# Fifteen of sixteen centroid rows in the table products of layers 1 and 2, and the attention weights loaded after the branch

## The chip, the cores and the metric

The kernel runs on one core of a Trainium2 chip. A core has five engines that run side by side, each through its own list of instructions in order: PE (TensorE, matrix products into PSUM), DVE (VectorE), ACT (ScalarE), POOL (GpSimd) and SP (SyncE, which here issues nearly all DMA transfers). They meet only at semaphores. The metric is the device time of one execution in microseconds (us). Before the change the median of three runs is 3867.28 us (3863.39 to 3868.2).

## The reference

The input x is 32 images of 1024 channels, 14 x 14 = 196 positions. Layer 0 is `x + L0(gn(x))`, and L0 is a chain of three table convolutions, each followed by a batch norm:

```python
scores = 2.0 * einsum('blcs,cks->blck', v, centroids) - sum(centroids * centroids, -1)
attn = softmax(scores * inv_temp, axis=-1)          # over the k = 16 centroids
out = einsum('blck,cko->blo', attn, lut)            # c codebooks, 16 table rows each
```

The first has 256 codebooks of 4 channels and 256 outputs, the second 256 codebooks of 9 values (the 3 x 3 neighbourhood of one channel) and 256 outputs, the third 64 codebooks of 4 channels and 1024 outputs. The 16 attention weights of a codebook add up to 1, so the sum over the 16 weighted table rows equals the last row plus the first fifteen weights times (row minus last row). The part that is the same at every position is taken out again by the mean in the batch norm that follows:

```python
m = x.mean((0, 2, 3), keepdims=True)
return g[None, :, None, None] * (x - m) * rsqrt(v + EPS) + b[None, :, None, None]
```

A second part, `x + L1(gn(x))`, is linear attention with rotated queries and keys and a 3 x 3 depthwise convolution. Everything is float32.

## The kernel before, in words

**Units.** Images go in NP = 16 pairs, 392 positions each. A unit is 64 codebooks of one pair: 4 blocks j of 128 rows (8 codebooks x 16 centroids), 8 units b to a pair, 128 units u = 8p + b to a layer. `units` (L626) is the loop of layers 1 and 2. In iteration i the program writes, in this order:

- `score(i + ahead)`: four score products on PE (L780 in layer 1; L897 and L906 in layer 2), and `exponentials` (L558) on ACT, which write the unit's tile t;
- `token_major` for the unit before that: DVE turns t into tt (L570); in layer 1 POOL adds its halves (L573);
- `softmax`: DVE sums (L587), inverts (L589) and turns the inverse back into r (L595), and POOL scales t by r (L596). In layer 1 (`halve`) this is unit i + 2, since ahead is 4; in layer 2 it is unit i + 2 as well, since ahead is 3;
- `side(i)`: what else is due in this iteration, from a list by iteration number;
- `lut(i)`: eight products on PE (L640), two halves h of the outputs times four blocks j, added up over the eight units of a pair. Each is two PE records.

Each engine keeps this order. The tiles t lie in a ring of ahead + 2 (`unit_tiles`, L616): six in layer 1, five in layer 2; unit u uses tile u modulo the ring's length.

**SP's queue.** Layer 1 loads x of a later pair (L247) once in eight units. In layer 2, `score2` issues the twelve patch loads of the next half pair (`load_patches`, L845) before the first unit of every four, into the one of two buffers that the last score products have left; `store_pair` (L825) writes six pieces of the padded activations once in eight units. A transfer that waits for a semaphore holds back all that follow it on SP.

**Tables.** `load_lut` fills one of eight tiles of 128 x 1024 (L237). Layer 1's are loaded at the start, layer 2's as the last pair of layer 1 leaves them, layer 3's likewise. After layer 3 the same tiles take the attention weights, wk (four tiles, the keys) and wq, in `projections`, called as `weights4` ahead of the branch.

**The branch.** The fast layers leave out the softmax's maximum; `overflow` (L602 to L608) checks that no sum left its range, and `tc.If(again > 0)` (L1036) repeats the layers exactly if one did. All engines meet there. With this input it isn't taken.

**The attention part** is written by a planner, `Plan`: each piece has an engine, a rank, an estimated duration and what it reads and writes, and at each free moment of an engine the ready piece of the lowest rank is emitted. `load` has the pieces for x (L1157) and for the third layer's output o3d (L1172); for the first pair the two x halves and the o3 pieces of half 1 were loaded before the branch (`given`). `front` and `group_norm` (L1192 to L1260) prepare the inputs, `channels` (L1318) multiplies by wk and wq.

Of the kernel before, what the change touches and what calls it, by code (L numbers as in the profile page):

```python
# [10 lines left out]
F32 = mybir.dt.float32  # L11
AF = mybir.ActivationFunctionType
ALU = mybir.AluOpType
# [4 lines left out]
P = 128  # L18
# [132 lines left out]
def conv_preact_kernel(ctx: ExitStack, tc: tile.TileContext, a: dict, out: bass.AP):  # L151
# [80 lines left out]
    def load_lut(b, src):  # L232

        v = weights[b]
        if len(src.shape) == 3:
            v = v.rearrange("p (s w) -> p s w", s=src.shape[1])
        nc.sync.dma_start(v, src)  # L237
        return v
# [120 lines left out]
    def score_biases(ps_tr, pool, tmp, i, raw, rows, groups, mask, per, order=None):  # L359
# [43 lines left out]

    lut1_rows = lambda b: a["lut1"][b * 512 : (b + 1) * 512].rearrange("(s q) w -> q s w", q=P)


    lut2_rows = lambda b: a["lut2"].rearrange("(h j b q) w -> h b q j w", h=2, j=4, q=P)[
        b // 4, b % 4
    ]

# [7 lines left out]
    def attention_inputs(stack):  # L418
# [61 lines left out]

        def projections(_):
            for b in range(8):
                t = a["wkT" if b < 4 else "wqT"]
                load_lut(b, t[(b % 4) * P : (b % 4 + 1) * P])

        return [loads, third, tables], projections, [third, projections]


    def layers(exact, early=None):
# [126 lines left out]
        def unit_tiles(pool, ahead):  # L616
# [6 lines left out]
            return ts  # L623

        def units(ahead, ts, pool, luts, score, bias, dst, stats, side, last, halve=False):

            n = 8 * NP
            po, late, tts = [], [], {}  # L630

            def lut(u):
                p, b = divmod(u, 8)
                if b == 0:
                    po[:] = [
                        ps_po.tile([P, 512], F32, tag="po", name="po")[:, :N2] for h in range(2)
                    ]
                order = [(h, j) for h in range(2) for j in range(4)]
                for h, j in order if b == 7 else sorted(order, key=lambda k: k[1]):
                    nc.tensor.matmul(  # L640
                        po[h],
                        luts[b][:, j, h * P : (h + 1) * P],
                        ts[u % len(ts)][:, j, :N2],
                        start=(b == 0 and j == 0),
                        stop=(b == 7 and j == 3),
                    )
                if b == 7:
                    for h in range(2):
                        o = dst[:, h, p * N2 : (p + 1) * N2]
                        nc.scalar.copy(o, po[h])  # L650
                        late.append((stats[:, h, p, :], o))

            for i in range(-ahead, n):
                u = i + ahead
                if u < n:
                    scs = score(u)
                    exponentials(ts[u % len(ts)], scs, bias[:, 4 * (u % 8) :][:, :4])
                u = i + ahead - 1
                if 0 <= u < n:
                    tts[u] = token_major(pool, ts[u % len(ts)], halve)  # L660
                u = u - 1 if halve else u
                if 0 <= u < n:
                    softmax(pool, u, ts[u % len(ts)], *tts.pop(u))
                while late:
                    nc.vector.bn_stats(*late.pop(0))
                side(i)
                if i >= 0:
                    lut(i)
            for h in range(2):
                nc.vector.bn_stats(*late.pop(0))  # L670
                last(h)
# [4 lines left out]
        with ExitStack() as s:  # L676
# [54 lines left out]

            luts2 = []

            def next_lut(b):
                return lambda: luts2.append(load_lut(b, lut2_rows(b)))

# [3 lines left out]
            at(24, edges)  # L740
            at(40, masks2)
            for b in range(7):
                at(8 * (NP - 1) + b + 1, next_lut(b))

            for p in range(2):
                xts[p] = load_x(xp, p)
            luts = [load_lut(b, lut1_rows(b)) for b in range(8)]
            if not exact:
                masks()
                load_consts(True)  # L750
            for i in (2, 3):
                load_raw(i)
            load_raw2()
            bias1, biases = score_biases(ps_tr, once, st, 1, raw[1], P, CT, mask8, 4)
# [19 lines left out]
            def score1(u):  # L774
# [12 lines left out]
                st,  # L787
                luts,
                score1,
# [6 lines left out]
            )  # L796
            next_lut(7)()
            add_up(0, 8 * NP)


        with ExitStack() as s:
            once = s.enter_context(tc.tile_pool(name="p2c", bufs=1))
            st = s.enter_context(tc.tile_pool(name="p2tt", bufs=1 if exact else 2))
            luts, luts3 = luts2, []

# [32 lines left out]
            def load_patches(n, b0=0, m=4):  # L838
                p, h = divmod(n, 2)
                for j in range(4):  # L840
                    for r0, dy, k in TAPS:
# [8 lines left out]
                        )  # L850

            store_pair(0, 0)
            load_patches(0, 0, 1)
# [63 lines left out]
            def side2(i):  # L917

                p = {1: 1}.get(i + ahead, (i + ahead + 9) / 8)
                if p in range(1, NP):  # L920
                    for h in range(2):
                        store_pair(int(p), h)
                if i == 60:
                    bias3, biases = score_biases(ps_tr, big, st, 3, raw[3], P, 2, mask8, 4)
                    parts[3] = score_matrices(big, 3, "", raw[3], mask8), bias3
                    biases()
                next_lut3(i - 8 * (NP - 1) - 1)

            def next_lut3(b):
# [9 lines left out]
                st,  # L939
                luts,  # L940
                score2,
# [89 lines left out]
    with tc.manual_schedule(engines=engines):  # L1031
        again = layers(False, early)
        weights4(None)

# [11 lines left out]
    with ExitStack() as s:  # L1046
# [102 lines left out]
        def load(p, h, rank):  # L1149
# [17 lines left out]
            for k in range(2):  # L1167
                ot = Slot("o3q")
                q = 2 * h + k

                def third(ot=ot, q=q):
                    nc.sync.dma_start(ot(), o3d[:, 2 * q : 2 * q + 2, p * N2 : (p + 1) * N2])  # L1172

                if p == 0 and h == 1:
                    ot.ap = given[f"o3_{k}"]
                else:
                    do(SP, rank - 11 + 8 * k, 0.45, third, (), [(ot, 0), (ot, 1)], lag=4.5)
                os.append(ot)
            return xt, os

        def front(p, h, c, xt, ot, rank):
# [34 lines left out]
            do(DVE, rank, 0.54, added, [w], [xk])  # L1216
            do(DVE, rank, 0.56, stats, [xk], [("gst", p % 2, h, c)])

        def group_norm(p, h, rank):
# [35 lines left out]
            def middle():  # L1255
# [11 lines left out]
            do(PE, rank, 0.3, average(pv, g("gq")), [key("gq")], [pv], lag=0.3)  # L1267
            do(DVE, rank, 0.1, variance, [pv], [key("gve")])
            do(
                POOL, rank, 1.9, scale, [key("gve"), key("nmc")], [key("ga"), key("gb")], port=True  # L1270
# [38 lines left out]
        def channels(p, keys, j, r, t, sums, rank):  # L1309
# [3 lines left out]
            pv = lambda: pq()[:, :N2]  # L1313

            def product():
                m0 = r * 512 + j * P
# [30 lines left out]
            done = ["wk"] if keys and p == NP - 1 else []  # L1347
            do(PE, rank, 2.76, product, ys_ + done, [pq, *held], lag=0.25)
            do(ACT, rank - 20, 0.49, relu, [pq], [e])
# [307 lines left out]
        def pair(p, t):  # L1657
# [51 lines left out]
            for n, j in enumerate(js):  # L1709
# [17 lines left out]
                if n % 2:  # L1727
                    store(p, j // 2, xts[j // 2], t + T + 40 + 20 * n)

        for p in range(NP):  # L1730
            pair(p, T * p)
# [74 lines left out]
```

## Time and profile before

| what | value |
|---|---|
| median of three runs | 3867.28 us |
| the profiled execution's own time | 3861.88 us |
| its span (first to last instruction) | 3860.0 us |
| PE busy | 3715.2 us, 96% |
| DVE busy | 3002.4 us, 78% |
| POOL busy | 2300.7 us, 60% |
| ACT busy | 1687.7 us, 44% |
| mean granted PE clock | 0.985 of full speed |

The instructions of layer 1 lie between 8 and 859 us of the span, those of layer 2 between 860 and about 1896, those of layer 3 up to 2665, then come the branch and the attention part. In the profile, L640 is line 640 of the kernel; `t<-t,lut` names the tiles written and read; a bracket at a line's end tells how long the engine was idle before it and what released it. Issuing a transfer does not count as busy time of SP. Several equal instructions in a row are merged in the timeline (x4), and the time given is from the first's start to the last's end. A busy PE is not a PE at its peak, as ends of products are modelled.

### The profile page before, as it was taken

To read this page: it belongs to the slowest core of one execution; us is meant where nothing else is said; L and a number is where in the kernel's file an instruction comes from. 1 tells how busy PE (TensorE), PEld (TensorE's weight loads), DVE (VectorE), ACT (ScalarE), POOL (GpSimd) and SP (SyncE) were. 2 spreads that over 40 slices of the span, in tenths; PEclk is the share of its full clock that TensorE was granted. 3 is DMA by queue.
4 is the path that set the end of the run, shared out by engine and by line. 5 is a ranking of instruction groups with operands and counts; after the bars stand their busy time and mean duration, and the time that the engine had idled before them with its cause. 6 is when DMAs were issued, how large, how long until landed. Compare 5 with 4: busy or idle time off the path is not lost. (4 is left out here: it accounts for less than half of the span.)

```text
span 3860.0 us, 45872 instructions
## 1 busy us (share of the span) xinstructions
PE 3715.2 (96%) x16415; PEld 2079.6 (54%) x16415; DVE 3002.4 (78%) x4281; ACT 1687.7 (44%) x3851; POOL 2300.7 (60%) x1338
## 2 busy tenths in 40 slices
PE   8999999999999999999999999995999999999998
PEld 5555555554555545555444444442666666666665
DVE  8999999978888888888633333332699999999996
ACT  4555555533333323333221222111766776666664
POOL 7999999974444444444311111110887888878886
PEclk9999999999999999999999999997999999999999
DMA  3111100015343333333111111103123223222221
GB/s 116 34 35 34 34 25 26 17 54 125 71 85 79 76 74 81 81 74 70 44 47 38 38 38 38 38 20 124 36 78 89 78 84 91 82 82 84 82 80 34
DMA packets 219107, 243.16 MB, mean 63 GB/s; under 512 B 24368, under 2 KB 216752, under 8 KB 218872
## 3 DMA queue, kind: packets, MB, share of 16 engines
q1 hardware_dynamic: 218296, 240.02, 23.3%
q8 instruction: 131, 2.15, 0.2%
q14 instruction: 104, 0.85, 0.1%
q10 hardware_dynamic: 576, 0.15, 0.0%
HBM read 163.55 MB, written 76.56 MB: 62 GB/s over the span
## 5 line engine op out<-in xcount | busy, mean ns | idle before, releaser
L596 POOL TENSOR_TENSOR t<-t,r 128x1664 f32<-128x1664 f32 (+1 forms) x284 | 1063.9, 3746 | 1188.3 <-DVE r L595 1153.8
L640 PE MATMUL po<-t,lut 128*128 128x392 f32 x4096 | 1418.1, 500 | 0.5 <-POOL t L596 0.5
L640 PEld LDWEIGHTS po<-t,lut 128*128 128x128 f32 x4096 | 759.9, 190 | 626.7 <-issue 123.7
L558 ACT ACTIVATE t<-sc,cbias 128x392 f32<-128x392 f32 (+1 forms) x1136 | 578.9, 592 | 1032.1 <-PE sc L906 646.6
L1318 PE MATMUL mm<-y,lut 128*128 128x392 f32 x2048 | 721.7, 500 | 4.8 <-DVE q L1335 2.9
L1005 PE MATMUL po<-t,lut 128*128 128x448 f32 x1792 | 682.2, 541 | 1.7 <-issue 1.7
L570 DVE STREAM_TRANSPOSE tt<-t 128x1664 f32<-128x1664 f32 (+1 forms) x284 | 544.3, 1917 | 167.8 <-ACT t L558 167.8
L595 DVE STREAM_TRANSPOSE r<-rc 128x1664 f32<-128x1664 f32 (+1 forms) x284 | 546.6, 1925 | 21.3 <-DVE rc L589 0.9
L1540 DVE SCALAR_TENSOR_TENSOR pa<-y,lepe_w,pa 128x406 f32<-128x406 f32 x900 | 540.7, 636 | 17.9 <-PE pa L1522 15.1
L1005 PEld LDWEIGHTS po<-t,lut 128*128 128x128 f32 x1792 | 339.0, 190 | 341.7 <-issue 341.5
L1318 PEld LDWEIGHTS mm<-y,lut 128*128 128x128 f32 x2048 | 375.7, 191 | 257.6 <-issue 14.3
L1014 DVE BATCH_NORM_STATS2 stats<-o 128x6 f32<-128x448 f32 x112 | 68.9, 617 | 487.5 <-ACT o L1013 487.5
L587 DVE TENSOR_REDUCE sm<-tt 128x104 f32<-128x832 f32 (+2 forms) x284 | 423.0, 1490 | 5.4
L573 POOL TENSOR_TENSOR tt<-tt 128x832 f32<-128x832 f32 x128 | 247.4, 1933 | 7.8 <-DVE tt L570 7.8
L1013 ACT COPY o<-po 128x448 f32<-128x448 f32 x112 | 59.0, 527 | 425.6 <-PE po L1005 381.2
L589 DVE RECIPROCAL rc<-sm 128x104 f32<-128x104 f32 (+1 forms) x284 | 229.5, 808 | 9.8
L897 PE MATMUL sc<-patch,cw 64*128 64x392 f32 x1024 | 210.4, 519 | 4.6 <-ACT t L558 2.5
L597 ACT ACTIVATE sm<-sm 128x104 f32<-128x104 f32 (+1 forms) x284 | 86.0, 303 | 177.1 <-DVE rc L589 176.9
L1503 POOL TENSOR_TENSOR qr<-qr,zb 128x784 f32<-128x784 f32 x64 | 117.6, 1850 | 70.2 <-DMA zb<-zd 68.2
L897 PEld LDWEIGHTS sc<-patch,cw 64*128 64x128 f32 x1024 | 90.5, 186 | 115.8 <-issue 74.2
L1327 ACT ACTIVATE e<-mm,kbd 128x392 f32<-128x392 f32 x128 | 74.1, 579 | 170.4 <-PE mm L1318 168.4
L1192 ACT ACTIVATE w<-x,tb,gn_a 128x196 f32<-128x196 f32 x248 | 128.2, 517 | 44.2 <-DVE tb L1061 20.9
(175 smaller groups left out, 3975.6 us busy)
## 6 DMA issues: line engine op xcount, KB each, us to landing
patch<-h1d SPq DMA_DIRECT2D x248, 162.8 KB
x<-in_x_dram SPq DMA_DIRECT2D x32, 784.0 KB
o3d<-o SPq DMA_DIRECT2D x14, 1792.0 KB
x<-in_x_dram SPq DMA_DIRECT2D x64, 392.0 KB
o<-o3d SPq DMA_DIRECT2D x64, 392.0 KB
out_dram<-x SPq DMA_DIRECT2D x64, 392.0 KB
h1d<-pad SPq DMA_DIRECT2D x96, 225.0 KB
patch<-h1d SPq DMA_DIRECT2D x124, 108.5 KB
```

Of the source, the lines that this page charges most:

```text
L558: nc.scalar.activation(t[:, j, : sc.shape[1]], sc, AF.Identity if exact else AF.Exp, bias=bias[:, j : j + 1],)
L570: nc.vector.transpose(tt, tf)
L573: nc.gpsimd.tensor_tensor(tv[:, :, :8], tv[:, :, :8], tv[:, :, 8:], ALU.add)
L587: nc.vector.tensor_reduce(sm, tv, AX.X, ALU.add)
L589: nc.vector.reciprocal(rc, sm)
L595: nc.vector.transpose(r, bc(rc, 2, KC))
L596: nc.gpsimd.tensor_tensor(tf, tf, r, ALU.mult)
L640: nc.tensor.matmul(po[h], luts[b][:, j, h * P : (h + 1) * P], ts[u % len(ts)][:, j, :N2], start=(b == 0 and j == 0), stop=(b == 7 and j == 3),
L897: nc.tensor.matmul(sc, w8[r, 8 * h + 4 * (j // 2) + g], grid(pbuf[n % NPB][r, j // 2, g]), start=True, stop=False,)
L1005: nc.tensor.matmul(po, luts[g][:, m * P : (m + 1) * P], t3[h][:, g % 4, :], start=(g == 0), stop=(g == 7),)
L1318: nc.tensor.matmul(pv(), w[kt][:, m0 : m0 + P], ywin(p, first + kt), start=(kt == 0), stop=(kt == 3),)
L1540: nc.vector.scalar_tensor_tensor(acc, neighbours(p, c, offset(k)), lw[:, c, k : k + 1], acc, ALU.mult, ALU.add,)
```

## The change

In layers 1 and 2 the table rows of centroid 15 are subtracted from the other fifteen, so that one row in sixteen of every block (partitions 15, 31, ..., 127) has nothing to do. Four units in a row, q = 0 to 3, form a group with 16 blocks and 15 remaining rows per codebook and block. Block j = 0 of a group's first unit is no longer multiplied by itself: its fifteen rows per codebook are placed in the free rows of the group's other fifteen blocks, on the table side once (`packed_lut`, `last_rows`) and on the attention side in every group (`spare_rows`): after the scaling L596 of a unit, SP copies rows of the first tile of the group into the free rows of this unit's tile, three transfers of 8 rows x 392 for q = 0 and four for the others, all inside SBUF. `lut` then leaves out j = 0 where b is 0 or 4.

The table of a unit is now made by two loads (`own`, `others`), four or five loads of repeated last rows into a second tile and one subtraction on POOL. In layer 1 the second tile is a part of out1 not yet in use; in layer 2 it is a pair of own tiles. The late constants and the centroids of layers 2 and 3 are loaded in iteration 16 instead of at the start.

The attention weights are loaded by eight pieces of the planner behind the branch, with the lowest ranks of SP but one, and the key and query products wait for their tiles. For the first pair, half 0, the output of layer 3 is loaded into buffers of qr instead of o3q, at the lowest rank. Two pieces of 16 and 10 products with the identity are added on PE around the group norm of the first pair, half 1.

In the repeated, exact layers (not run here) the same is done, with the first tile's rows kept in DRAM.

```diff
+    def packed_lut(layer, b):
+        rows, spare = unit_rows(layer, b), unit_rows(layer, b - b % 4)[0]
+        j0 = 0 if b % 4 else 1
+        k0 = 4 * (b % 4) + j0 - 1
+        v = weights[b].rearrange("p (s w) -> p s w", s=4)
+        def own():
+            nc.sync.dma_start(v[:, j0:], rows[j0:].rearrange("j c k w -> (c k) j w"))
+        def others():
+            nc.sync.dma_start(v[15::16, j0:], spare[:, k0 : k0 + 4 - j0])
+        return v, own, others
+
+    def last_rows(d, layer, b):
...
+        for j in range(j0, 4):
+            nc.sync.dma_start(d[:, j], rows[j][:, 15:].to_broadcast([8, KC, W]))
+        nc.sync.dma_start(d[15::16, j0:], spare[:, 15:].to_broadcast([8, 4 - j0, W]))
+        def less():
+            nc.gpsimd.tensor_tensor(v[:, j0:], v[:, j0:], d[:, j0:], ALU.subtract)
+        return less
...
+        def spare_rows(ts, u):
+            q = u % 4
+            t, first = ts[u % len(ts)], ts[(u - q) % len(ts)][:, 0, :N2]
+            if exact:
...
+            for j in range(0 if q else 1, 4):
+                nc.sync.dma_start(t[15::16, j, :N2], first[4 * q + j - 1 :: 16])
...
-                order = [(h, j) for h in range(2) for j in range(4)]
+                j0 = 0 if b % 4 else 1
+                order = [(h, j) for h in range(2) for j in range(j0, 4)]
...
                     softmax(pool, u, ts[u % len(ts)], *tts.pop(u))
+                    spare_rows(ts, u)
...
+            for b in range(8):
+                at(b - 5 if b > 1 else -99, lambda b=b: luts[b][2]())
+                if b > 1:
+                    at(b - 6, lambda b=b: load_last(b))
+                at(b - 2 if b > 1 else -99, lambda b=b: lasts[b]())
...
+                if i == -ahead:
+                    luts2[7][2]()
+                    for b in range(2):
+                        load_last(b)
+                for b in range(8):
+                    if i == max(b - 2, 1 - ahead):
+                        without_last(b)
...
         again = layers(False, early)
-        weights4(None)
...
-                ot = Slot("o3q")
+                ot = Slot("qr" if p == 0 and h == 0 else "o3q")
...
-                    do(SP, rank - 11 + 8 * k, 0.45, third, (), [(ot, 0), (ot, 1)], lag=4.5)
+                    r = rank - 11 + 8 * k if p > 0 else -99
+                    do(SP, r, 0.45, third, (), [(ot, 0), (ot, 1)], lag=4.5)
...
+                for n, need in ((16, []), (10, [key("gve")])):
+                    warm(n, need)
...
+            need = [("w", b) for b in (range(4) if keys else range(4, 8))]
...
-            do(PE, rank, 2.76, product, ys_ + done, [pq, *held], lag=0.25)
+            do(PE, rank, 2.76, product, ys_ + done + need, [pq, *held], lag=0.25)
...
+        for b in range(8):
+            do(SP, b - 90, 0.95, weights4[b], (), [("w", b)], lag=3.5 + b)
```

## The prediction

> **What bounds the kernel now.** I read the page first. PE is busy 96% of the span, and the table products (L640) are its largest group: 1418.1 us for 4096 records, 0.346 us each, two records to one 128x392 product.
>
> ```profile
> L640 PE MATMUL po<-t,lut 128*128 128x392 f32 x4096 | 1418.1, 500 | 0.5 <-POOL t L596 0.5
> L596 POOL TENSOR_TENSOR t<-t,r 128x1664 f32<-128x1664 f32 (+1 forms) x284 | 1063.9, 3746 | 1188.3 <-DVE r L595 1153.8
> ```
>
> PE almost never waits for the attention weights that POOL finishes in L596. Next the busy time by stretch (columns: PE, PEld, DVE, ACT, POOL, clock, DMA share, GB/s), one stretch in layer 1 and one in layer 2:
>
> ```profile
> 200.00:700.00 500.00, 500.00 (x1941) 262.01 (x1940) 480.90 (x551) 254.48 (x641) 465.19 (x178) 1.00 0.11 33
> 1000.00:1200.00 200.00, 200.00 (x821) 100.51 (x821) 169.00 (x109) 64.72 (x165) 93.09 (x25) 1.00 0.38 81
> ```
>
> Layer 1 is PE bound, but DVE stands at 96% and POOL at 93%: there is hardly a second resource to spare. Layer 2 has DVE at 84% and POOL at 47%. A unit takes 6.34 us in layer 1 and 7.85 us in layer 2 (distance of consecutive L640 starts). The busy share does not tell whether a unit's tile can be reused in time, so I read the timeline. Layer 1, near its end:
>
> ```profile
> 800.50 2.02 ACT L558 ACTIVATE t<-sc,cbias 128x392 f32<-128x392 f32 x4 [3.23 <-PE sc L780]
> 801.89 3.72 POOL L596 TENSOR_TENSOR t<-t,r 128x1664 f32<-128x1664 f32 x1 [0.55 <-DVE r L595]
> 802.55 1.91 DVE L570 STREAM_TRANSPOSE tt<-t 128x1664 f32<-128x1664 f32 x1 [0.80 <-ACT t L558]
> 806.83 2.02 ACT L558 ACTIVATE t<-sc,cbias 128x392 f32<-128x392 f32 x4 [3.17 <-PE sc L780]
> 821.04 3.72 POOL L596 TENSOR_TENSOR t<-t,r 128x1664 f32<-128x1664 f32 x1 [0.81 <-ACT t L558]
> ```
>
> Following the program order, the exponentials at 800.50 belong to a unit n, the product at 801.89 to n-2, that at 821.04 to n+1. So the exponentials of n+1 (806.83) start only 1.2 us after the scaling of n-2 ends (805.61). Layer 2:
>
> ```profile
> 1646.66 2.02 ACT L558 ACTIVATE t<-sc,cbias 128x392 f32<-128x392 f32 x4 [5.57 <-PE sc L906]
> 1648.71 1.91 DVE L570 STREAM_TRANSPOSE tt<-t 128x1664 f32<-128x1664 f32 x1 [1.17 <-ACT t L558]
> 1652.93 7.01 SPq L845 DMA_DIRECT2D patch<-h1d  x12
> 1655.54 3.72 POOL L596 TENSOR_TENSOR t<-t,r 128x1664 f32<-128x1664 f32 x1 [4.13 <-DVE r L595]
> 1663.40 3.72 POOL L596 TENSOR_TENSOR t<-t,r 128x1664 f32<-128x1664 f32 x1 [4.13 <-DVE r L595]
> 1670.22 2.02 ACT L558 ACTIVATE t<-sc,cbias 128x392 f32<-128x392 f32 x4 [5.56 <-PE sc L906]
> ```
>
> Call w the last unit (q = 3) of a group of four. The first two lines and 1655.54 are unit w-1, 1663.40 is w, 1670.22 is w+2. SP issues twelve patch loads at 1652.93; in stretches of 1 us the DMA share is about 0.8 until it falls to 0.39 at 1665 and 0 at 1666: 12.5 us from first issue to last byte. With the six stores ahead (1563.20, 4.35 us of issue) the burst lasts until 1580.6, 17.4 us. Then the branch:
>
> ```profile
> 2662.56 4.33 SPq L237 DMA_DIRECT2D lut<-in_wkT_dram  x4
> 2665.49 0.17 DVE L329 TENSOR_TENSOR bi<-bn_b,bi 128x8 f32<-128x8 f32 x1
> 2682.15 1.74 POOL L1075 MEMSET y<- 128x128 f32 x7 [17.10 <-SPq L1036]
> ```
>
> Compute ends at 2665.7; all engines stand until the weights have landed (bytes flow until about 2680).
>
> **What the Trainium skill says.** DMA: Bandwidth & Descriptors, section Anatomy of one DMA: about 2.0 us fixed per transfer whatever its size (given for the GpSimd path; here SP issues), and a semaphore wait is held on the issuing sequencer before dispatch. The trace agrees: the 16 KB mask issued at 0.72 releases DVE at 2.72, and SP shows waits of 583.5 us at L247, in its order. Same page, section Queues, rings and completion order: each engine consumes its ring of a queue in order. Section Why a DMA increments its semaphore by 16 and not by 1: an 8-partition transfer uses the 8 lowest engines. No transfer of that shape is in this trace.
>
> **The change, part by part.**
>
> *Products removed.* Each group of four units drops one 128-row block for both halves: 2 of 32 products, 4 x 0.346 = 1.39 us. Per group PE falls from 25.35 to 23.96 us (layer 1) and from 31.4 to 30.0 us (layer 2). 64 groups: 88.6 us if PE stays the bound. In layer 1 DVE needs 0.962 x 25.35 = 24.4, so at most 1 us per group could ever be had there.
>
> *Spare rows.* After each scaling, 3 or 4 transfers inside SBUF, each from the group's first tile; the unit's products wait for them. The four issue at about 0.4 us each (0.33 to 0.45 in the trace for small ones) and the last lands 2.0 to 2.6 us after its issue: D = 3 x 0.4 + 2.2 = 3.4 us after the scaling. Bounds: 2.0 (one fixed cost) to 5.0 (0.6 us per issue, slow landing). PE is not the one hurt: in layer 1 it reads a tile 6 us after its scaling, in layer 2 11 us. The new wait is on reuse. The first tile of group v..v+3 is read by the transfers of v+3; in layer 1 (six tiles) ACT overwrites it for v+6, one iteration later in the program, in layer 2 (five tiles) for v+5. DVE's transpose of that unit stands behind it, and every softmax behind that.
>
> *Layer 1.* The loop that sets the pace is: exponentials of v+6, two DVE iterations, DVE up to r of v+7, scaling, transfers, exponentials of v+10. One DVE iteration is 1.9 + 0.98 + 0.8 + 1.91 and gaps = 5.7 us. So 2.05 + 5.7 + 5.7 + 5.65 + 0.15 + 3.72 = 23.0, with two group-norm statistics (1.1 each) in one group of a pair and one 1.0 in the other: 25.2 + D and 24.0 + D. (Check: 800.50 to 824.76 is 24.3 with 1.4 us of DVE idle and one 1.0.) At D = 3.4 eight units take 56.0 against 50.7: +5.3, times 15.5 = +82. The wait is free only to D = 0.75. PE no longer trails at the end (8.9 us after the last scaling instead of 11.3): -2. Layer 1: **+80**.
>
> *Layer 2.* Here D up to about 3.1 us is free (1670.22 against 1667.12), but SP's order is: transfers of w-1, then (in every second group the six stores and) twelve patch loads, then transfers of w. Before, the loads went out at 1652.93; now they wait for the scaling of w-1 (1659.26), plus 1.7 us for its own transfers. 12.5 us later the loads have drained, and the transfers of w land 1.2 us after: 15.4 us behind the scaling of w-1, 19.8 to 20.3 with stores. Then exponentials and start of the transpose 2.1, one DVE iteration 6.7, and that unit (the next w-1) ends its scaling 10.55 us after its transpose began (1648.71 to 1659.26). Sum: 15.4 + 2.1 + 6.7 + 10.55 = 34.8 per group, 39.6 with stores; 74.4 against 62.9 for both: +11.5, times 15 pairs = +172. If only SP's issue time counted (1.7 + 7.0 + 3.2 = 11.9): 31.3 and 35.7, +4 a pair, +62. Last-row loads at its start (8 x 5 transfers, 512 KB a unit, between the first patch loads): +8. At its end PE trails less: -7. Layer 2: **+173**.
>
> *Packing the tables.* Subtraction on POOL, 128x1024: 3.72 x 1024/1664 = 2.3 us, six of them in the first iterations of layer 1, where POOL has 0.4 to 1.3 us of room: +6. The first two stand ahead of POOL's first L573 (28.06) and wait for 1 MB more of loads, until about 29 + 4: +5. In layer 2 POOL's idle half hides them; the constants moved to iteration 16 are needed only at a layer's end, 800 us later. **+11**.
>
> *Weights behind the branch.* The last store of the products (issued 2661.92) has its bytes through at about 2668; restart took 2.1 us after the last byte, so 2670 instead of 2682: -12. Its residual load now goes first into a qr buffer: the 2.5 us that DVE waited for o at 2693: -2. The weights, 4 MB, take some 12 us after restart and the first key products come 20.9 us after it (2703.04), so they stay hidden; without that cover 5 us. The warm-up products run while PE idles. **-14**.
>
> Sum on the profiled execution (3861.88 us, span 3860.0): 3861.9 + 80 + 173 + 11 - 14 = 4112. The median of runs lies 5 us above that execution, hence 4115.
>
> **Rivals.**
> 1. *SP's order alone counts* (the small transfers pass the patch loads on the DMA engines): 4112 - 110 = 4002. For: eight short rows ask little of an engine. Against: the ring order.
> 2. *Slow small transfers*, D = 5 in layer 1 (+50) and 2 us more per group in layer 2 (+60): 4222. Nothing in the trace shows it.
> 3. *Ends faster: transfers are short and overtake.* Layer 2 keeps its 44.5 us if D stays under 3.1 there, and layer 1 with D = 2.0 costs 2.5 x 15.5 - 2 = 37: 3862 - 44 + 37 + 11 - 14 = 3852. It decides at D = 2.3 in layer 1; with D near 0 the whole intent comes out, layer 1 gaining 0.75 x 31 = 23: 3792. Against: four issues alone exceed 1.2 us.
>
> **How the numbers follow.** Likeliest 0.68 (own range 4050 to 4180), SP's order alone 0.16, slow transfers 0.08, overtaking 0.08. The range 3990 to 4205 holds the likeliest and rival 1; rival 3 and most of rival 2 stay out. Changes under 0.2% (8 us) can't be told from none. Rival 3 is split between faster and within 0.2%: 0.06 and 0.02.
>
> **What would show it.** Right: L558 waiting for a DMA once in four units in both layers; layer-1 groups of about 28 us, layer-2 groups alternating near 35 and 40; L570 idle for L558; PE under 90% busy in both layers, with 3840 L640 records; restart near 10 us after L329. Wrong: L640 back to back in layer 2 at 7.5 us a unit would overturn the queueing step; layer-1 groups under 25.3 us would overturn the reuse step.

## The result and the profile after

The changed kernel takes 4220.17 us (median of 4 runs, 4218.61 to 4233.35), against 3865.55 for the kernel before in the same comparison: ratio 1.0928, 95% interval 1.0906 to 1.0950. It is slower, as forecast, but by 355 us where the forecast had 248. The profiled execution has a span of 4218.3 us. The answers to the lines shown of before, from the page (out<-in, count | busy, mean ns | idle before, releaser):

```profile
L693 PE MATMUL po<-t,lut 128*128 128x392 f32 x3840 | 1384.6, 515 | 34.9 <-DMA t<-t 32.5
L630 POOL TENSOR_TENSOR t<-t,r 128x1664 f32<-128x1664 f32 (+1 forms) x284 | 1063.0, 3743 | 1441.2 <-DVE r L629 1313.4
L592 ACT ACTIVATE t<-sc,cbias 128x392 f32<-128x392 f32 (+1 forms) x1136 | 579.9, 593 | 1390.6 <-DMA t<-t 684.7
L604 DVE STREAM_TRANSPOSE tt<-t 128x1664 f32<-128x1664 f32 (+1 forms) x284 | 540.7, 1904 | 550.6 <-ACT t L592 501.8
```

The last two groups in the kernel before:

```profile
L558 ACT ACTIVATE t<-sc,cbias 128x392 f32<-128x392 f32 (+1 forms) x1136 | 578.9, 592 | 1032.1 <-PE sc L906 646.6
L570 DVE STREAM_TRANSPOSE tt<-t 128x1664 f32<-128x1664 f32 (+1 forms) x284 | 544.3, 1917 | 167.8 <-ACT t L558 167.8
```

The products lost 256 records, as intended, and wait only 32.5 us for the copies. Who waits is ACT: most of its idle time ended with score products of PE, and now 684.7 us of it end with a transfer of t to t. DVE, behind it, waits 501.8 us for ACT where it waited 167.8. The same two kinds of stretch as before (PE, PEld, DVE, ACT, POOL, clock, DMA share, GB/s):

```profile
200.00:700.00 500.00, 441.92 (x1651) 228.85 (x1651) 426.48 (x487) 226.62 (x568) 411.54 (x159) 0.95 0.12 36
1400.00:1600.00 200.00, 171.37 (x652) 86.34 (x648) 133.46 (x87) 51.40 (x130) 78.39 (x22) 0.92 0.33 75
```

No engine is full any more, and PE's granted clock is 0.95 and 0.92 where it was 1.00. The timeline of the kernel after in layer 1, around the fourth unit of a group:

```profile
500.15 3.72 POOL L630 TENSOR_TENSOR t<-t,r 128x1664 f32<-128x1664 f32 x1 [0.76 <-DVE r L629]
503.90 2.57 SPq L675 DMA_DIRECT2D t<-t  x4
507.89 2.02 ACT L592 ACTIVATE t<-sc,cbias 128x392 f32<-128x392 f32 x4 [8.31 <-DMA t<-t]
509.95 1.91 DVE L604 STREAM_TRANSPOSE tt<-t 128x1664 f32<-128x1664 f32 x1 [2.37 <-ACT t L592]
```

The scaling ends at 503.87, the exponentials that overwrite the group's first tile start at 507.89: D is 4.0 us, 2.6 for issuing the four copies and 1.4 after that. In layer 2, a group without stores (the twelve patch loads stand in SP's queue between two units' copies; the first four of the seven copies are those of the group's last unit):

```profile
1542.07 3.72 POOL L630 TENSOR_TENSOR t<-t,r 128x1664 f32<-128x1664 f32 x1 [2.86 <-DVE r L629]
1548.43 6.82 SPq L929 DMA_DIRECT2D patch<-h1d  x12
1555.84 5.92 SPq L675 DMA_DIRECT2D t<-t  x7
1563.11 2.02 ACT L592 ACTIVATE t<-sc,cbias 128x392 f32<-128x392 f32 x4 [14.81 <-DMA t<-t]
```

From the scaling's end (1545.79) of the unit before the last to the exponentials 17.3 us pass. The start of the program:

```profile
27.46 5.29 SPq L424 DMA_DIRECT2D lut<-in_lut_dram  x6
32.79 1.25 SPq L427 DMA_DIRECT2D lut<-in_lut_dram  x2
39.19 4.10 POOL L442 TENSOR_TENSOR lut<-lut,out 128x768 f32<-128x768 f32 x2 [16.71 <-DMA lut<-in_lut_dram]
43.44 3.71 DVE L604 STREAM_TRANSPOSE tt<-t 128x1664 f32<-128x1664 f32 x2 [17.14 <-POOL t L655]
```

The first two subtractions wait for spare rows that SP issues behind the loads of six other tables; DVE's first transpose, at 26.1 before, waits for fills (L655) that POOL has behind the subtractions. At the start of layer 2:

```profile
1038.75 0.62 SPq L439 DMA_DIRECT2D drop<-in_lut_dram  x1
1039.41 2.49 SPq L438 DMA_DIRECT2D drop<-in_lut_dram  x4
1045.29 0.61 SPq L439 DMA_DIRECT2D drop<-in_lut_dram  x1
1094.04 2.02 ACT L592 ACTIVATE t<-sc,cbias 128x392 f32<-128x392 f32 x4 [34.90 <-DMA drop<-in_lut_dram]
```

L439 overwrites rows that L438 has just written, so SP stands from 1041.90 to 1045.29 until those have landed, and the copies behind it stand too. Such waits of L439 add up to 65 us over the program (34.2 in layer 1's tables, 31.0 in layer 2's). The exponentials at 1094.04 had then stood for 34.9 us; by the program they wait for copies of t, which SP issues behind these loads. The branch:

```profile
3058.33 0.17 DVE L329 TENSOR_TENSOR bi<-bn_b,bi 128x8 f32<-128x8 f32 x1
3063.36 1.76 POOL L1166 MEMSET y<- 128x128 f32 x7 [5.47 <-DVEq L1127]
```

It takes 4.9 us where it took 16.5. By stage (first table product, last output copy of each layer, last L329, first key product): start 38.0 to 57.0, layer 1 821.1 to 937.9, layer 2 1037.0 to 1294.1, layer 3 769.6 to 769.5, to the first key product 37.3 to 23.6, attention 1157.0 to 1136.2. The last is 21 us that no step of the prediction had.

### The profile page after: what moved, and what is told of

It reads as the page before. It is cut to its first block, busy times and chain, and to the rows that moved or that the text cites. A ratio compares the mean times of both kernels' runs of the same rounds, so it can differ in the third digit from the quotient of the medians.

```text
span 4218.3 us, 48505 instructions
## 1 busy us (share of the span) xinstructions
PE 3773.6 (89%) x16211; PEld 2104.8 (50%) x16211; DVE 2979.3 (71%) x4281; ACT 1690.4 (40%) x3851; POOL 2336.8 (55%) x1354
## 5 line engine op out<-in xcount | busy, mean ns | idle before, releaser
L693 PE MATMUL po<-t,lut 128*128 128x392 f32 x3840 | 1384.6, 515 | 34.9 <-DMA t<-t 32.5
L592 ACT ACTIVATE t<-sc,cbias 128x392 f32<-128x392 f32 (+1 forms) x1136 | 579.9, 593 | 1390.6 <-DMA t<-t 684.7
L693 PEld LDWEIGHTS po<-t,lut 128*128 128x128 f32 x3840 | 736.4, 197 | 665.5 <-issue 193.1
L604 DVE STREAM_TRANSPOSE tt<-t 128x1664 f32<-128x1664 f32 (+1 forms) x284 | 540.7, 1904 | 550.6 <-ACT t L592 501.8
L1097 PEld LDWEIGHTS po<-t,lut 128*128 128x128 f32 x1792 | 339.0, 190 | 341.8 <-issue 341.5
L982 PE MATMUL sc<-patch,cw 64*128 64x392 f32 x1024 | 268.4, 609 | 195.6 <-ACT t L592 192.2
L982 PEld LDWEIGHTS sc<-patch,cw 64*128 64x128 f32 x1024 | 128.2, 214 | 313.0 <-ACT t L592 221.6
L607 POOL TENSOR_TENSOR tt<-tt 128x832 f32<-128x832 f32 x128 | 247.7, 1935 | 66.0 <-DVE tt L604 65.9
L854 PE MATMUL sc<-x,cw 32*128 32x392 f32 x1024 | 134.7, 576 | 95.0 <-ACT x L761 91.9
```

The costliest lines, as they stand in the source:

```text
L592: nc.scalar.activation(t[:, j, : sc.shape[1]], sc, AF.Identity if exact else AF.Exp, bias=bias[:, j : j + 1],)
L604: nc.vector.transpose(tt, tf)
L607: nc.gpsimd.tensor_tensor(tv[:, :, :8], tv[:, :, :8], tv[:, :, 8:], ALU.add)
L693: nc.tensor.matmul(po[h], luts[b][:, j, h * P : (h + 1) * P], ts[u % len(ts)][:, j, :N2], start=(b == 0 and j == j0), stop=(b == 7 and j = ...
L982: nc.tensor.matmul(sc, w8[r, 8 * h + 4 * (j // 2) + g], grid(pbuf[n % NPB][r, j // 2, g]), start=True, stop=False,)
L1097: nc.tensor.matmul(po, luts[g][:, m * P : (m + 1) * P], t3[h][:, g % 4, :], start=(g == 0), stop=(g == 7),)
```

## The experiments

The diffs are in short form. `e_rings`, `e_order`, `e_both` and `e_twice` were run once each. Theory A was the prediction's: the reuse of a group's first tile waits for the last copies from it, and SP's order makes these late in layer 2. The rival B: the copies are slow for the products that need them, and neither tile nor place matters. "Group" is the distance between DVE's transposes (L604) four units apart.

**Which tile, and which place in the queue.** `e_rings`:

```diff
+def tile_of(ts, u):
+    g, q = divmod(u, 4)
+    return ts[g % 2] if q == 0 else ts[2 + (3 * g + q - 1) % (len(ts) - 2)]
-ts[u % len(ts)]
+tile_of(ts, u)
```

> The changed kernel with one edit: which tile a unit of weights takes. The first unit of each group of four alternates over two tiles that are kept for first units; the other three units rotate over the rest. There are as many tiles as before (six in layer 1, five in layer 2), but the tile of a first unit is written again only eight units later. Theory A (the reuse of the first unit's tile after the last copies from it sets the group): layer 1 falls from about 28.4 to 24.5-25 us a group, layer 2 from about 38.8 (mean of 36.6 and 41.0) to about 32; 30 groups of 3.5 us and 30 of 6.5 us are about 300 us less: near 3920 us. Theory B (the products wait for the copies that write, or the transfers themselves are what is slow, whichever tile they read): 4220 us, within 20.

Measured: 3934.37 us, against 3848.19 for before on the same chip. Layer 1 has 24.8 to 25.1 us a group, layer 2 30.1 and about 36 in turn. The exponentials of `e_rings` at the same place:

```profile
515.98 2.02 ACT L592 ACTIVATE t<-sc,cbias 128x392 f32<-128x392 f32 x4 [1.01 <-PE sc L862]
523.56 2.02 ACT L592 ACTIVATE t<-sc,cbias 128x392 f32<-128x392 f32 x4 [2.06 <-issue]
```

Neither waits for a transfer. With the same copies at the same places, two tiles for first units take 289 us away (from the 4223.14 of `e_after_pf`, below).

`e_order`:

```diff
-if g == 0 and n + 1 < 2 * NP: load_patches(n + 1)      # in score2
+if g == 0 and n + 1 < 2 * NP: due.append(n + 1)
+while due: load_patches(due.pop())                     # in side2, behind the copies
```

> The changed kernel with one edit: in layer 2 the twelve patch loads of a group are issued behind the copies of the group's fourth unit, where they stood ahead of them. The six stores stay where they are. Theory A (SP's order in time, patch loads ahead of copies, is what makes the copies late): the groups of layer 2 fall from 36.6 and 41.0 to about 30.5 and 33-35 us, layer 1 stays at 28.4: near 4030 us. Theory B (SP's queue is not what layer 2 waits for): 4220 us, within 20.

Measured: 3991.84 us; layer 1 as before the edit, layer 2 29.5 to 31.0 us a group. The patch loads now come after the copies, and the wait is D again. The groups with stores, for which A had 33 to 35 us, take at most 1.5 us longer than the others, so the stores by themselves hold up little. The scaling ends at 1515.22, the exponentials start 3.9 us later (timeline of `e_order`, layer 2):

```profile
1511.50 3.72 POOL L630 TENSOR_TENSOR t<-t,r 128x1664 f32<-128x1664 f32 x1 [3.78 <-DVE r L629]
1517.88 7.98 SPq L929 DMA_DIRECT2D patch<-h1d  x12
1519.09 2.02 ACT L592 ACTIVATE t<-sc,cbias 128x392 f32<-128x392 f32 x4 [8.28 <-DMA t<-t]
```

`e_both` has the two edits together.

> The changed kernel with the two edits together: first units on two tiles of their own, and the patch loads behind the copies. Theory A: nothing of the copies is left on the path; layer 1 at 24.5-25 us a group, layer 2 at about 30 (TensorE bound); what is left above the kernel before is the packing of the tables: 3880 to 3920 us. Theory B: 4220 us.

Measured: 3876.81 us (this one and `e_order` with an attention of 1152.5 and 1150.0, which is explained further down); layer 1 24.8 to 25.1, layer 2 30.1 in all but the first three groups and the one of iteration 60, which has the third layer's preparation (39.3 us in before). B falls with these three.

**The cost of one copy.** `e_twice`:

```diff
 nc.sync.dma_start(t[15::16, j, :N2], first[4 * q + j - 1 :: 16])
+nc.sync.dma_start(t[15::16, j, :N2], first[4 * q + j - 1 :: 16])
```

> The changed kernel with every spare-row copy issued twice (the second writes the same values). Theory A (issue on SP plus landing lies on the path of every group): each group of layer 1 grows by about 4 issues of 0.65 us, 2.6 us, and layer 2 by 2.6 to 5 us a group: 60 groups, +160 to +230 us, near 4400 us. Theory B (issue time is off the path): 4220 us, within 20.

Measured: 5302.84 us, 900 more than A said. I had overlooked that the second copy writes what the first writes, so SP holds it until the first has landed. SP's queue:

```profile
580.27 0.56 SPq L675 DMA_DIRECT2D t<-t  x1
581.97 0.57 SPq L676 DMA_DIRECT2D t<-t  x1
582.60 0.56 SPq L675 DMA_DIRECT2D t<-t  x1
```

This measures one copy by itself: 1.70 us from the start of its issue to the issue that waited for it. A pair takes 2.33 us, the 15 of a group 35 us, and layer 1 goes to about 41 and 47 us a group in turn; SP's waits at the second copies add up to 1220 us. As a test of the size of A's term it is spoiled; it shows all the more that SP's queue can set the pace.

**The branch part alone** (the kernel before with the weights behind the branch, the qr slots, the warm-up products), and without the warm-up products:

```diff
+for b in range(8):                                      # e_branch
+    do(SP, b - 90, 0.95, weights4[b], (), [("w", b)], lag=3.5 + b)
-for n, need in ((16, []), (10, [key("gve")])):          # e_branch_cold
-    warm(n, need)
```

> The kernel before with one part of the change alone: the eight key and query weights loaded behind the branch, two o3 slots in the buffer of qr, the warm-up products, the wait of each product for its weights. The tables and their products are those of before. The prediction's term is -14 us (restart 12 earlier, first key product 2 more): 0.4% below before. The two traces put it at -35: -12 at the restart, -2 to the first key product, and 21 us less from there to the end, which the prediction did not have. Theory A (the 21 us belong to the branch part): 0.9% below. Theory B (they come from something else in the changed kernel): 0.4% below.

> The same branch part without the 26 warm-up products. Theory A1 (the warm-up products give the 21 us): 0.4% below before. Theory A2 (they come from the new slots and places of the transfers in the planned order): 0.9% below before, as with them.

Measured against a before of 3848.62 us: `e_branch` 3845.5 us, ratio 0.9986 (0.9979 to 0.9993); `e_branch_cold` 3851.24 us, 1.0007 (0.9998 to 1.0015). Neither theory: 0.1% where 0.4 or 0.9% was expected. Yet in the trace of `e_branch` the first key product comes 23.7 us after L329, which is the whole -14. The rest is elsewhere: its attention takes 1152.8 us, in the trace of after 1136.2.

**The fills at the start.** `e_memset`:

```diff
+ts1 = unit_tiles(once, AHEAD)
 side(-AHEAD - 1)
 ...
-unit_tiles(once, AHEAD),
+ts1,
```

> The changed kernel with one statement moved: the tiles of weights of layer 1 are made, and their padding filled by GpSimd, ahead of the first two subtractions of last rows, not behind them. Theory A (the 17 us at the start are VectorE's first transpose waiting for these fills, which queue behind the subtractions): the first transpose goes back from 43 to about 26 us, the first table product waits for the subtractions (43.3) instead of 57.0: 13 us less, ratio to the changed kernel 0.997. Theory B (the start is set by the tables' transfers alone): no difference.

Measured: 4227.29 us, ratio to before 1.0983 (1.0964 to 1.1001). The timeline of its start:

```profile
26.34 1.91 DVE L604 STREAM_TRANSPOSE tt<-t 128x1664 f32<-128x1664 f32 x1 [2.18 <-ACT t L592]
38.22 4.10 POOL L442 TENSOR_TENSOR lut<-lut,out 128x768 f32<-128x768 f32 x2 [17.20 <-DMA lut<-in_lut_dram]
42.28 3.79 POOL L607 TENSOR_TENSOR tt<-tt 128x832 f32<-128x832 f32 x2
```

The transpose is back at 26.3, but POOL's halve adds (L607) stand behind the same subtractions, and the first product comes at 53.8, 3 us earlier instead of 13. A was right on the first wait and blind to the next. This run also had an attention of 1149.8 us, from the same source text of that part as after's 1136.2.

**The order of visits.** `Plan.write` visits the engines in the order of a Python set of their names, which the source does not fix. The traces of after and `e_memset` have the attention's instructions in two orders. So I fixed the order in the kernel before:

```diff
-engines = {p[0] for p in self.pieces}
+engines = dict.fromkeys(("POOL", "DVE", "PE", "ACT", "SP"))    # e_pool_first
+engines = dict.fromkeys(("DVE", "POOL", "PE", "ACT", "SP"))    # e_dve_first
```

> The kernel before with one line of the planner fixed: it visits the engines in the order GpSimd, VectorE, TensorE, ScalarE, SyncE; in the kernel before the order is that of a Python set, which differs from one build to the next. The traces of the changed kernel and of e_memset have the attention's instructions in two different orders from one source text, 1136 and 1150 us long. Theory A (the visiting order sets the length of the attention, and the change has no part in it): the attention falls to 1135-1140 us where GpSimd is visited ahead of VectorE. Theory B (the attention's length comes from the chip or from what goes before it): the same as e_dve_first, within 3 us.

> The same with VectorE visited ahead of GpSimd. Theory A: the attention takes 1150-1160 us, the whole 15 to 20 us longer than e_pool_first (0.4 to 0.5%). Theory B: no difference between the two.

Measured: 3848.93 us, ratio 1.0000 (0.9991 to 1.0009), attention 1140.8; and 3862.29 us, 1.0036 (1.0021 to 1.0050), attention 1154.2. The before of these comparisons (3849.61 us here) has no trace of its own; by its time it agrees with POOL first. The before shown in this document, 3867 us with an attention of 1157.0, is DVE first: from the first key product on, its trace has the same sequence of instructions on every engine as that of `e_dve_first`. After has the sequence of `e_after_pf` (below), which is POOL first; on PE, DVE and POOL, `e_order`, `e_both`, `e_branch`, `e_branch_cold`, `e_memset` and `e_best` share another one. One group shows the two orders at a glance (DVE's groups by shape in the attention; busy, mean ns), here that of `e_pool_first`:

```profile
L1450 DVE TENSOR_TENSOR kmm<-ks,hmean 128x32 f32<-128x32 f32 x32 | 10.6, 349 | 0.0
```

And the same group of `e_dve_first`:

```profile
L1450 DVE TENSOR_TENSOR kmm<-ks,hmean 128x32 f32<-128x32 f32 x32 | 24.6, 801 | 0.0
```

The same 32 instructions take 14 us more where they fall at other moments. What they meet there was not tried, nor whether these 14 us are the 13 by which the attentions differ. With POOL first, the branch part again (`e_branch_pf`):

> The kernel before with the branch part alone, GpSimd visited first. Against e_pool_first. Theory A (the branch part is worth what the restart shows, and the 21 us of the attention were the visiting order): 14 us below e_pool_first, 0.36%. Theory B (the 21 us belong to the branch part): 35 us below, 0.9%.

Measured: 3833.75 us, ratio 0.9959 (0.9945 to 0.9973), 15 us below `e_pool_first`; to the first key product 37.6 became 23.7. So 13 of the 21 us in the attention are the order of visits (1154.2 to 1140.8; 12.7 between `e_branch` and `e_branch_pf`). The other 8 are not explained: among the kernels with the sequence of after, the attention takes from 1135.9 to 1143.9 us. The warm-up products have a share: `e_branch` and `e_branch_cold`, both with the longer attention (1152.8 and 1155.7), differ by 5.7 us in the medians, and their intervals do not meet.

**What the packing costs.** Four kernels with POOL first: the changed one; one that leaves out the loads of the last rows and their subtraction together; one with the late constants spread over iterations 12 to 32; and one that leaves out the copies, and so one sixteenth of the rows.

```diff
-at(16, later)                       # e_spread
+for k, f in enumerate(rest):
+    at(12 + k, f)
-spare_rows(ts, u)                   # e_nocopy, in the fast layers
-nc.sync.dma_start(d[:, j], ...)     # e_nopack: these loads,
-nc.gpsimd.tensor_tensor(v[:, j0:], v[:, j0:], d[:, j0:], ALU.subtract)   # and this
```

> The changed kernel with GpSimd visited first by the planner, as the one to compare the next three with. Its profile has the attention at 1136 us, so this is the same program order: about 4210 on a chip where before is 3849.

> The changed kernel (GpSimd first) without the loads of last rows and without their subtraction: the tables are loaded and their spare rows filled, but nothing is subtracted, so the sums lack that term. Theory A (these loads on SP and their waits are most of the miss outside the loops): start 13 to 17 us earlier, the first groups of layer 1 down by about 10, those of layer 2 from 70.2 and 44.8 to about 42 and 40: 50 to 70 us below e_after_pf. Prediction's term: 11 to 19 us.

> The changed kernel (GpSimd first) with the late constants and centroid loads issued one at a time over iterations 12 to 40 in place of all at iteration 16. Theory A (they stand in SP's queue ahead of the copies): the group of 42.5 us at iteration 16 falls to about 28.5, and nothing else changes: 14 us below e_after_pf. Prediction's term: nothing.

> The changed kernel (GpSimd first) without the copies of spare rows: the sums lack one sixteenth of their rows; packing and branch as in the changed kernel. Theory A (the copies cost what the two loops show, about 84 us in layer 1 and 213 in layer 2, and the products removed are worth 1 to 1.3 us a group): layer 1 at about 25 us a group, layer 2 at 30.1 with the slow first groups left: 290 to 310 us below e_after_pf, near 3910. Theory B (without copies TensorE's saving shows in full, 88 us): near 3840.

Measured (one run each, before 3850.49): 4223.14, 4156.19, 4216.73 and 3815.22 us. The first is 13 us above what was expected, the last below both of its theories. By stage of the trace, in us:

| stage | e_pool_first | e_after_pf | e_nopack | e_spread | e_nocopy |
|---|---|---|---|---|---|
| start to first table product | 38.2 | 55.8 | 41.4 | 57.0 | 55.4 |
| layer 1 | 821.2 | 939.0 | 926.7 | 927.3 | 804.7 |
| layer 2 | 1037.2 | 1297.4 | 1255.5 | 1295.6 | 1020.1 |
| layer 3 | 769.6 | 769.5 | 769.1 | 771.1 | 769.5 |
| to first key product | 37.6 | 23.7 | 23.0 | 24.9 | 23.5 |
| attention | 1140.8 | 1135.9 | 1138.7 | 1139.0 | 1139.9 |
| span | 3844.6 | 4221.3 | 4154.4 | 4214.9 | 3813.1 |

The last rows cost 14 us at the start, 12 in layer 1 and 42 in layer 2, whose first groups fall from 68.6 and 46.4 to 36.6 and 41.5. How much of this is SP's waiting and how much POOL's work, this run does not part. The constants cost 12 us in layer 1 (the group of 42.6 becomes 29.9); the run shows 6.4, with 5 us more in other stages, less than the 15 us by which runs of the changed kernel differ. The copies cost 408 us, more than A's 290 to 310. A had counted from the groups of the kernel before; without copies layer 1 runs at 24.9 and layer 2 at 30.1 us a group, faster than before by 0.9 and 1.3, and the slow first groups fall too (68.6 to 34.5 in layer 2, 42.6 to 25.0 at iteration 16), which fits that a queue on SP hurts less when no copy stands in it. TensorE's full 88 us (B) do not show: 31 groups of 0.9 and 31 of 1.3 us are 68. 3849 less these and less 14 for the branch is 3767; the rest to 3815, 48 us, is by this estimate what packing still costs there.

**A version that keeps what works.** `e_best` has tiles and patch loads as in `e_both`, the fills ahead, and the packing rescheduled; `e_best_pf` is the same with POOL first. `e_best2_pf` changes two places of it more:

```diff
 luts[b][1](); load_last(b)          # b = 0, 1; then their spare rows and L439; then 2 to 7
 at(b - 6, load_last(b))
+at(b - 5, lasts[b][0])              # L439, one iteration behind L438
-at(16, later)
+at(12 + k, f)                       # one of the late loads an iteration
-bufs=2
+bufs=3                              # last-row tiles of layer 2
-at(8 * p - 17, load(p))             # e_best2_pf: x of pair 2 ahead of that packing,
+at(8 * p - 17 if p > 2 else -99, load(p))
-if b > 1 and i == b - 4: load_last(b)                    # and L438 at an iteration's
+if u - ahead == max(b - 4, 1 - ahead): load_last(b)      # start, not at its end
```

> The changed kernel with first units on two tiles of their own, patch loads behind the copies, the fills of the start ahead of the subtractions, and the packing rescheduled so that SP waits less in its queue: the load that overwrites rows of the last-row tile is issued one iteration after the loads it overwrites, the first two tables' own loads come ahead of the other six, the late constants go one at a time over iterations 12 to 40 in place of all at 16, in layer 2 the patch loads stand ahead of the second-half tables' spare rows and the last-row tile has three buffers. Theory A (what e_both has left above before is queueing of the packing on SP and GpSimd): 70 to 100 us below e_both: 3775 to 3810 where before is 3848, about 1.5% faster than before. Theory B (the packing's transfers and subtractions cost the same wherever they stand): as e_both, 0.7% slower than before.

> e_best with GpSimd visited first. Theory A: 15 us below e_best, near 3825 us; against e_pool_first 22 to 26 us below, 0.6%. Theory B: as e_best, 3840 us.

> e_best_pf with two moves more: in layer 2 the loads of a last-row tile are issued at the start of an iteration, so that a unit's copies lie between them and the load that overwrites part of the tile; in layer 1 the third pair of x is loaded ahead of the packing of the tables 2 to 7, not among it. Theory A (what is left of the packing is SP waiting in its queue): layer 2's first groups go from 39.5, 46.9, 38.3 to about 34, 36, 32, layer 1's first from 37.6 to about 30: 25 to 35 us below e_best_pf, near 3800, 1.3% below before. Theory B (the subtractions and transfers cost this wherever they stand): 3831, no difference.

Measured: `e_best` 3839.87 us, ratio 0.9974 (0.9965 to 0.9983), `e_best_pf` 3831.31 us, 0.9953 (0.9936 to 0.9969), `e_best2_pf` 3808.05 us, 0.9879 (0.9862 to 0.9896), 1.2% faster than before. The branch part alone brings 15 of these 41 us (`e_branch_pf`). `e_best` missed its 3775 to 3810, for two reasons at least. It was built with DVE first (attention 1158.8), though POOL first brought only 9 of the expected 15 us in the runs. And its first groups of layer 2 stayed at 39.0, 49.8 and 37.3 us, because L439, "one iteration later" in the program, stood directly behind L438 in SP's queue: an iteration's end is next to the following one's start (in this kernel L439 is line 441):

```profile
897.53 2.63 SPq L438 DMA_DIRECT2D drop<-in_lut_dram  x4
904.30 0.62 SPq L441 DMA_DIRECT2D drop<-in_lut_dram  x1
```

`e_best2_pf` puts a unit's copies between them. SP's waits at this load in layer 2 fall from 22.2 us (`e_best_pf`) to 5.8, with the same subtractions on POOL, and layer 2 takes 1022.6 us where it took 1037.5; its first groups are 40.3, 39.4 and 30.1. Layer 1, which has the other move, takes 800.9 us where it took 808.3. The two together brought 23 us, a little less than the expected 25 to 35, and both layers are now close to those of `e_nocopy`. The products' group of `e_best2_pf`:

```profile
L709 PE MATMUL po<-t,lut 128*128 128x392 f32 x3840 | 1340.1, 502 | 41.2 <-DMA t<-t 29.8
```

78 us less than before's 1418.1, of which 41 us at most return as waits.

## Why the prediction was right or wrong

Direction and mechanism were right, and the sum was too small. Built with one visiting order the change costs 376.7 us of span (3844.6 to 4221.3), where the prediction's terms add to 250. Of the 127 us between them about 62 are the packing, which is the step that failed, 52 layer 2 and 14 layer 1. By its steps:

- *Products removed*: right. Without copies a group takes 30.1 us in layer 2 (predicted 30.0) and 24.9 in layer 1, where DVE was said to stop it at 24.4 (24.8 with the right base, see below).
- *Spare rows*: the wait was named rightly (ACT, once in four units, on reuse of the first tile), and `e_rings` shows it. The size: D is 4.0 us, not 3.4. The issues follow each other at 0.67 us, where the prediction took 0.4; the last lands, and ACT starts, 2.0 us after its issue began, where it took 2.2.
- *Layer 1*: 28.4 us a group against 28.0. After the packing (12.3) and the constants (11.7) are taken off its 117.8 us, 94 are left against +80. D at 4.0 makes that 19 more. But the base was read too low, and this hid most of it: 6.34 us is most units' distance, two in eight take 6.8, so eight units of the kernel before take 51.6 us and not 50.7, which makes it 13 less. Some 9 of the 94 us have no term.
- *Layer 2*: the order on SP is the cause (`e_order`), but groups take 36.6 and 41.0 us (means) against 34.8 and 39.6. The leg from the scaling of w-1 to the landing is 17.3 us, not 15.4: own copies 2.6 instead of 1.7 before the first patch load, and 14.7 instead of 13.7 from there. 30 groups with 1.4 to 1.9 us more: of 260.2 us, less 41.9 of packing and 1.8 that `e_spread` took, 217 against 165 (173 less its +8 for the start).
- *Packing the tables*: this step failed. +11, and +8 in layer 2, were 69 us of last rows and 12 of constants. It priced POOL's instructions and the bytes. It did not see that L439 waits on SP for L438 (65 us in all), so that everything behind it in that queue waits; that POOL's fills and halve adds queue behind the first two subtractions; that the spare rows these need are issued behind six other tables. "Needed only at a layer's end" was true of the constants' users and beside the point: 29 small loads, 18.6 us of issue from 201.62 on, stood ahead of the copies on SP.
- *Weights behind the branch*: -14 predicted, -13.9 in the trace, -15 in the runs. Its sign "restart near 10 us" did not fit its own sum, which has 4.5; it took 4.9.

Rival 1 (issue time alone, 31.3 and 35.7 us) falls: in the group shown of layer 2 the last unit's four copies are issued by 1559.06, and the exponentials start 4.0 us after that, against 1.4 in layer 1. The transfers do wait behind the patch loads, as the Trainium skill's DMA: Bandwidth & Descriptors has it in Queues, rings and completion order: each DMA engine takes up descriptors in ring order. Rival 2 had 4222, nearest to the result, by luck: D is 4.0, not 5, so most of its +50 in layer 1 is not there; its 2 us more a group in layer 2 is about right, and other misses, the packing above all, made up the rest. Rival 3 falls with D above 2.3. The range ended at 4205, and no rival had a larger cost of the packing. (Two slips carry nothing: the last addition, 4112 and 5, is 4117; and transfers to eight partitions were in its trace, the sixteen centroid loads of L532.) The comparison also gained 13 us from the order of visits, without which the range would have been missed by more.

## What to carry to other kernels

When a change adds transfers to a queue that waits in order, write down that queue's whole order with every wait in it, write-after-write waits between the new transfers included, before pricing bytes or engine time; and count "one iteration apart" in the queue, not in the program. Look whether a tile that becomes the source of late copies can have a ring of its own: here the number of tiles stayed the same and 289 us went. Before a few tenths of a per cent are given to an edit, make sure that an order which the source leaves open is the same on both sides.

## What the runs showed of the hardware

- A copy of 8 rows of 1568 bytes inside SBUF takes 1.70 us from the start of its issue until a transfer that waits for it is issued (`e_twice`). The Trainium skill (DMA: Bandwidth & Descriptors, Anatomy of one DMA) has about 2.0 us fixed, for the GpSimd path, where these are issued by SP; SP spends about 0.65 us on each when it issues four in a row.
- PE's granted clock is lower where PE waits often: in the stretches shown it is 1.00 with PE busy all the time, 0.95 at 88% and 0.92 at 86%; over the whole of `e_twice` it is 0.863. The products' records take 0.361 us after (1384.6 / 3840), 0.346 before and 0.349 in `e_best2_pf`, so part of the saving seems to be paid back where something else stalls. The two were seen together; no run varied the clock alone.
- The same 128x32 operation on DVE takes 349 or 801 ns in the mean (`e_pool_first`, `e_dve_first`), by what is written around it. The cause is open.
